# Four stacked graph-attention layers on one core: the instruction order planned anew, with other assumed durations for DMA transposes and ScalarE copies and with new due times for all layers

## The chip, the core and the metric

The kernel runs on one core of a Trainium2 chip. The metric is the device time of one execution in microseconds, the median of several runs. The engines are named as in the profile: PE (TensorE matmuls), PEld (its weight loads), DVE (VectorE), ACT (ScalarE), POOL (GpSimd) and SP (SyncE, which here only issues DMAs).

## What is computed

The input `x` has 16 batches of 1024 nodes with 256 features; `adj` is one 1024 x 1024 adjacency matrix for all of them. Four layers follow each other, each with a norm in front and a residual behind:

```python
# each layer:
h = jnp.maximum(_layernorm(x, axis=-1), 0.0)
x = x + layer(h, adj)
# layers 0 and 3 (4 heads of 64) and layer 1 (1 head of 256):
q = h @ W
e = leaky_relu(q @ a_src [node j] + q @ a_dst [node i], 0.2)   # 1024 x 1024 a head
out = elu(softmax(where(adj > 0, e, -big)) @ q)
# layer 2:
e = leaky_relu((h @ W1) @ (h @ W2).T, 0.2)
out = relu(softmax(where(adj > 0, e, -big)) @ (h @ W3))
```

Batches are independent of each other; the layers of one batch are not.

## The kernel before

**How the work is cut.** Nodes lie in 8 tiles of 128 (`NT`), queries in two halves of 512 (`HALF`). The exponential of a sum is a product, so in layers 0, 1 and 3 no 1024 x 1024 exponential is taken: a factor for each key (`ke`) and a row of factors for all queries (`row`) are combined on DVE by one instruction for 128 keys and 512 queries, which also applies the mask and gives the tile `p`. That is `weigh`, L1109 in layers 0 and 3 (64 tiles a batch and layer: 2 halves x 4 heads x 8 key tiles) and L1200 in layer 1 (16 tiles). PE then multiplies `p` with the values. In layers 0 and 3 (`steps_a`) each `p` is used by one PE step of 8 matmuls into the tile `acc`; in layers 1 and 2 (`steps_b`) a PE step takes all 8 key tiles of a half for one tile of queries, 16 matmuls into `accb`. Layer 2 computes scores on PE (`score`), takes two exponentials on ACT (`grow`, L1227 and L1228) and combines and masks on DVE (`cut`, L1232 and L1233). All matmuls in f32 go through `product`, so they all have line L575; the profile tells them apart by the tile that they write: `acc`, `accb`, or `pp` for projections, queries and scores.

After an `acc` is complete, DVE takes the reciprocal of its denominators (L1142) and the division frees the `acc`: in layer 0 on ACT (L1156), in layer 3 mostly on DVE (L1153). There are two buffers each of `acc` and `accb`, 8 of `p` for layers 0 and 3, and 18 of `p1` for layers 1 and 2.

**The way into a layer** (`prologue`). DVE takes the mean and variance of each tile of `x` (`statistics`, L815 and L816); eight such pairs belong to a batch and layer. The reciprocal root is a POOL instruction (L851) between two small ones on DVE (L848, L854). For each pair of tiles ACT then normalises (`normed`, L884, 2 instructions) and splits the f32 into two 16-bit planes (`split`, L907, 2 instructions); SP issues one DMA transpose (`move`, L911); ACT joins the planes again (`kept`, L925); PE projects (`projected`, `pp<-w,hTp` or `pp<-w2v,hT`); ACT evicts (`evict`, L960 to L969). In layers with 4 heads that aren't `filling`, DVE scales the values (L975). The factors of a layer are turned on PE (`factors`), stored to DRAM and read back as broadcast rows by SP's DMAs (L1043, L1056). The buffers between these steps are few: 4 of `h`, 2 of `planes`, 2 of `turned`, 2 of `hTp`, 4 of `pp`.

**What sets the order.** The program is laid out by a small planner, `Plan`. Each step is added with an engine, an assumed cost, a due time, the steps that it needs, and the buffers that it takes and gives. `Plan.order` (L95) plays the steps through on paper: whenever an engine is idle, it takes the ready step with the earliest due time whose buffers are free. The order in which it picks them is the order in which the instructions are emitted, so each engine's queue follows it. Costs and due times therefore change nothing but the order. The due time of a step comes from these tables (L49 to L66): `START` (when a layer of batch 0 begins, in units of `PERIOD`; batch b is b units later), `LEAD` and `AHEAD` (how much earlier the way into the layer is due), `STEP` (spacing of its four pairs of tiles), `WHEN` (layers 1 and 2: start and spacing for the tiles and for the products), `LATER` (shifts of single batches and layers), `EARLY` (how much earlier the divisions are due). Layers of neighbouring batches are in work together: in the middle of the run, layer 0 of one batch goes with layers 1, 2 and 3 of the batches before it.

The step of the DMA transpose is four plan steps, of which `landed` (L616) adds the last two:

```python
s = plan.add(ACT, 1.25, at, split, (s,), take=("planes",), give=("h", "h"))   # L932
s = plan.add(SP, 0.5, at, move, (s,), take=("turned",))
s = landed(s, at, 256, give=("planes",))         # DMA: 256 / 330 us, then LAND: 2.2 us
s = plan.add(ACT, 1.02, at, kept, (s,), take=take, give=("turned",))
```

Of the kernel before, what the change touches and what calls it, by code (L numbers as in the profile page):

```python
# [45 lines left out]

PERIOD, EARLY = 190.0, 0.74  # L49
START = {0: 0.0, 1: 0.96, 2: 2.3, 3: 3.63}  # L50
LEAD = {0: 0.7841, 1: 0.4991, 2: 0.193, 3: 1.8815}
STEP = {0: 0.028, 1: 0.0997, 2: 0.0747, 3: 0.0167}
WHEN = {
    (1, "weights"): ((-0.3, 0.04), (-0.12, 0.06)),
    (1, "attended"): ((0.56, 0.06), (0.22, 0.15)),
    (2, "weights"): ((-0.04, 0.02), (0.31, 0.02)),
    (2, "attended"): ((0.72, 0.07), (0.79, 0.02)),
}

LATER = {  # L60
    (0, 0): -0.048, (0, 1): -0.131, (1, 0): 0.06, (1, 1): 0.875, (2, 0): 0.05, (13, 2): -0.063, (13, 3): 0.612,
    (14, 2): 0.069, (14, 3): 0.042, (15, 2): -0.05, (15, 3): 1.076,
}
AHEAD = {
    (1, 0): 0.853, (2, 0): 0.078, (3, 0): 0.177, (13, 0): -0.55, (15, 2): -0.107, (15, 3): -0.22,
}  # L66


PE, DVE, ACT, POOL, SP, DMA, LAND = "PE", "DVE", "ACT", "POOL", "SP", "DMA", "LAND"
# [463 lines left out]
def fast(  # L533
# [26 lines left out]
    plan = Plan(bufs, ("p", "p1", "acc", "accb", "val4", "val1", "x", "row4", "row1"))  # L560
# [55 lines left out]
    def landed(step, due, kb, take=(), give=()):  # L616

        s = plan.add(DMA, kb / 330, due, lambda: None, (step,))
        return plan.add(LAND, 2.2, due, lambda: None, (s,), give=give)
# [133 lines left out]
    weights = ((w0, w0_ready), (w1, w1_ready), (w2v, w2v_ready), (w3, w3_ready))  # L753
# [67 lines left out]
    class Layer:  # L821
# [7 lines left out]
        def prologue(self, due, step, stats, direct=False):  # L829
# [3 lines left out]
            b, heads, layer = self.b, self.heads, self.layer  # L833
# [6 lines left out]
            ready = []  # L840
            parts = PARTS[b == 0] if direct else ((0, NT),)
            for n, its in enumerate(slice(*part) for part in parts):
# [29 lines left out]
                at = due - (len(parts) - n - 1)  # L872
                s = plan.add(DVE, 0.2, at, norm, (*stats[its], ready[-1] if n else None))
                s = plan.add(POOL, 2.0, at, norm2, (s,))
                take = () if n else (tag,) if self.gat else (tag, "hq")
                ready += [plan.add(DVE, 0.2, at, norm3, (s,), take=take)] * (its.stop - its.start)
            copies, evicted = [], []
            for n, t0 in enumerate(range(0, NT, 2)):
                at = due + n * step
# [9 lines left out]
                            scale=T["rstd"][:, t : t + 1],  # L889
                        )  # L890

                s = plan.add(ACT, 1.2, at, normed, (ready[t0],), take=("h", "h"))


                def turned(t0=t0):
# [31 lines left out]
                take = ("hTp",) if self.gat else ()  # L927
                if direct:
                    s = plan.add(PE, 0.47, at, turned, (s,), take=("pp",), give=("h", "h"), wide=True)
                    s = plan.add(ACT, 0.6, at, kept, (s,), take=take, give=("pp",))  # L930
                else:
                    s = plan.add(ACT, 1.25, at, split, (s,), take=("planes",), give=("h", "h"))  # L932
                    s = plan.add(SP, 0.5, at, move, (s,), take=("turned",))
                    s = landed(s, at, 256, give=("planes",))
                    s = plan.add(ACT, 1.02, at, kept, (s,), take=take, give=("turned",))
                copies.append(s)
                for k in range(2):
                    t = t0 + k

                    def projected(t=t, t0=t0, k=k):  # L940
                        pv = T["pv", t] = buf("pp", [P, HALF])
                        for c in range(KC):
                            product(
                                pv[:, :cols],
                                T["hT", t0][:, c, k * P : (k + 1) * P],
                                w[:, c, :cols],
                                start=(c == 0),
                                stop=(c == KC - 1),
                            )

                    s2 = plan.add(
                        PE, 0.9, at + (k + 1) * step / 3, projected, (s, w_ready), take=("pp",),
                        give=("hTp",) if k and self.gat else (),
                    )

                    def evict(t=t, many=heads > 1 and (direct or not self.filling)):
                        to = self.val[:, t, :, :d]
                        of = T["pv", t][:, :F].rearrange("p (h d) -> p h d", h=heads)
                        if not self.gat:
                            nc.scalar.copy(to, of)  # L960
                            return
                        a = self.val[:, t, :, d : d + 1]

                        nc.scalar.activation(
                            a, T["pv", t][:, F + heads : cols].unsqueeze(2), AF.Exp, scale=1.0 / (SLOPE - 1.0)
                        )
                        nc.scalar.activation(self.ke[:, :, t], T["pv", t][:, F:cols], AF.Exp)
                        for hd in range(0 if many else heads):
                            nc.scalar.mul(to[:, hd, :], of[:, hd, :], a[:, hd, :])  # L969

                    def scaled(t=t):
                        to = self.val[:, t, :, :d]
                        of = T["pv", t][:, :F].rearrange("p (h d) -> p h d", h=heads)
                        a = self.val[:, t, :, d : d + 1]
                        nc.vector.tensor_mul(to, of, a.to_broadcast([P, heads, d]))  # L975

                    many = heads > 1 and (direct or not self.filling)
                    cost = 0.4 if many or not self.gat else 0.8 if heads == 1 else 1.15
                    s2 = plan.add(ACT, cost, at, evict, (s2,), give=() if many else ("pp",))
                    if many:  # L980
                        s2 = plan.add(DVE, 0.43, at, scaled, (s2,), give=("pp",))
                    evicted.append(s2)
            at = due + 4 * step
            self.ready, self.queries = evicted, ([], [])
            if not self.gat:
                for dc in range(KC):
                    for n0 in range(0, N, HALF):
# [12 lines left out]
                        s = plan.add(PE, 1.72, at, query, (*copies, *w12_ready), take=("pp",))  # L1000
# [8 lines left out]
            if direct:  # L1009
                for half in range(2):  # L1010
                    for hd in range(heads):
# [7 lines left out]
                        def keep(half=half, hd=hd):  # L1019
# [5 lines left out]
                            take=("pp", f"row{heads}"), wide=True,  # L1025
# [20 lines left out]
            s = plan.add(PE, 0.14, at, factors, tuple(evicted), take=("pp",))  # L1046
# [141 lines left out]
    def steps_b(lay, dues):  # L1188

        T = {}  # L1190
        ready = {0: [], 1: []}
        for n in range(2 * NT):
            half, jt = divmod(n, NT)
            at = dues("weights", n)
            after = (lay.ready[jt], *mask_ready[half, jt // HT])
            if lay.gat:

                def weigh(half=half, jt=jt):
                    p = T["p", half, jt] = buf("p1", [P, HALF])
                    nc.vector.scalar_tensor_tensor(  # L1200
                        p, lay.rows[half, 0], lay.ke[:, 1, jt : jt + 1], mask_of(half, jt), op0=OP.max, op1=OP.mult
                    )

                s = plan.add(
                    DVE, 0.67, at, weigh, (*after, lay.row_ready[half, 0]), take=("p1",),
                    give=("row1",) if jt == NT - 1 else (),
                )
                ready[half].append(s)
                continue

            def score(half=half, jt=jt):
                e = T["e", half, jt] = buf("pp", [P, HALF])
                for c in range(KC):
                    product(
                        e,
                        lay.hT[:, c, jt * P : (jt + 1) * P],
                        lay.qT[:, c, half * HALF : (half + 1) * HALF],
                        start=(c == 0),
                        stop=(c == KC - 1),
                    )  # L1220


            def grow(half=half, jt=jt):
                e = T.pop(("e", half, jt))
                p = T["p", half, jt] = buf("p1", [P, HALF])
                u = T["u", half, jt] = buf("u", [P, HALF])
                nc.scalar.activation(u, e, AF.Exp, scale=1.0 - SLOPE)  # L1227
                nc.scalar.activation(p, e, AF.Exp, bias=shift_col, scale=SLOPE)  # L1228

            def cut(half=half, jt=jt):  # L1230
                p, u = T["p", half, jt], T.pop(("u", half, jt))
                nc.vector.scalar_tensor_tensor(p, u, 1.0, p, op0=OP.max, op1=OP.mult)  # L1232
                nc.vector.tensor_mul(p, p, mask_of(half, jt))  # L1233

            s = plan.add(PE, 1.72, at, score, (*lay.queries[half], *mask_ready[half, jt // HT]), take=("pp", "p1"), give=("hq",) if n == 2 * NT - 1 else ())
            s = plan.add(ACT, 1.2, at, grow, (s,), take=("u",), give=("pp",))
            ready[half].append(plan.add(DVE, 1.27, at, cut, (s,), give=("u",)))
        for it in range(NT):
            half, t = divmod(it, HT)
# [227 lines left out]
```

## Time and profile before

Three runs took 3021.66, 3022.22 and 3024.54 us; the median is 3022.22 us. The profiled execution has a span of 3023.1 us and a mean granted PE clock of 0.993.

| engine | busy us | share of the span | instructions |
|---|---|---|---|
| PE | 2929.2 | 97% | 47954 |
| DVE | 2632.4 | 87% | 5286 |
| ACT | 1926.1 | 64% | 4776 |
| POOL | 225.7 | 7% | 151 |

Busy time is the union of an engine's instructions. For PE the difference to the span, 93.9 us, is time in which no matmul runs; short gaps between pipelined matmuls don't count as idle. The profile names for each stretch of idle time the instruction that ended it. The costliest groups are L1109 (2048 instructions, 1450.8 us busy) on DVE, and on PE the products into `acc` (32768 matmuls), into `accb` (8192) and into `pp`. One DMA transpose keeps SP's queue for 1.23 us (median of 248).

### The profile page before, as it was taken

To read this page: it belongs to the slowest core of one execution; us is meant where nothing else is said; L and a number is where in the kernel's file an instruction comes from. 1 tells how busy PE (TensorE), PEld (TensorE's weight loads), DVE (VectorE), ACT (ScalarE), POOL (GpSimd) and SP (SyncE) were. 2 spreads that over 40 slices of the span, in tenths; PEclk is the share of its full clock that TensorE was granted. 3 is DMA by queue.
4 is the path that set the end of the run, shared out by engine and by line. 5 is a ranking of instruction groups with operands and counts; after the bars stand their busy time and mean duration, and the time that the engine had idled before them with its cause. 6 is when DMAs were issued, how large, how long until landed. Compare 5 with 4: busy or idle time off the path is not lost.

```text
span 3023.1 us, 108612 instructions
## 1 busy us (share of the span) xinstructions
PE 2929.2 (97%) x47954; PEld 2248.8 (74%) x47954; DVE 2632.4 (87%) x5286; ACT 1926.1 (64%) x4776; POOL 225.7 (7%) x151
## 2 busy tenths in 40 slices
PE   7899999999999999999999999999999999999997
PEld 5775888768686786867868687787867869685686
DVE  7988869989898898988979898899988979896698
ACT  6677686675656756567675656756567675547633
POOL 2110000000100000000000100001000000100000
PEclk9899999999999999999999999999999999999999
DMA  4232223213222232322323223231322323121210
GB/s 141 59 68 64 51 58 97 71 44 86 46 72 56 62 76 44 84 42 71 73 46 83 45 62 72 54 83 42 84 44 71 73 47 69 33 57 40 51 41 24
DMA packets 344047, 188.06 MB, mean 62 GB/s; under 512 B 268880, under 2 KB 304400, under 8 KB 343568
## 3 DMA queue, kind: packets, MB, share of 16 engines
q1 hardware_dynamic: 343152, 180.51, 25.9%
q8 instruction: 378, 6.19, 0.9%
q14 instruction: 101, 0.83, 0.1%
q10 hardware_dynamic: 416, 0.52, 0.1%
HBM read 98.63 MB, written 17.33 MB: 38 GB/s over the span
## 4 chain that ended last, share of the span: by engine, by line
PE 82%; DVE 14%; ACT 2%; issue 1%; DMA 0%; SPq 0%; DVEq 0%; ACTq 0%
PE pp L575 30%; PE accb L575 26%; PE acc L575 26%; DVE p L1109 8%; DVE bn L815 2%; DVE o L1080 1%; DVE mv L816 1%; DVE xt L1082 1%; DVE p L1200 1%; ACT o L1156 0%; DMA xt<-in_x_dram 0%; ACT hTp L925 0%; DVE p L1233 0%; ACT ex L1076 0%; ACT ex L1075 0%
## 5 line engine op out<-in xcount | busy, mean ns | idle before, releaser
L1109 DVE SCALAR_TENSOR_TENSOR p<-row,ke,mask 128x512 f32<-128x512 f32 x2048 | 1450.8, 762 | 69.6 <-PE acc L575 63.0
L575 PEld LDWEIGHTS acc<-val,p 128*64 128x64 f32 x32768 | 1072.9, 139 | 156.7 <-DVE p L1109 52.9
L575 PE MATMUL acc<-val,p 128*64 128x65 f32 x32768 | 1085.7, 224 | 56.9 <-DVE p L1109 45.0
L575 PE MATMUL accb<-val,p 128*64 128x257 f32 x8192 | 932.9, 380 | 0.4 <-ACT o L1265 0.4
L575 PEld LDWEIGHTS accb<-val,p 128*64 128x64 f32 x8192 | 700.2, 137 | 159.3 <-issue 3.9
L575 PE MATMUL pp<-qT,hT 128*64 128x512 f32 x2048 | 458.1, 592 | 0.0
L575 PE MATMUL pp<-w,hTp 128*64 128x264 f32 (+1 forms) x3072 | 381.1, 390 | 6.5 <-ACT hTp L925 5.4
L575 PEld LDWEIGHTS pp<-qT,hT 128*64 128x64 f32 x2048 | 149.6, 137 | 237.7 <-issue 230.9
L575 PEld LDWEIGHTS pp<-w,hTp 128*64 128x64 f32 x3072 | 240.6, 139 | 93.2 <-issue 11.4
L884 ACT ACTIVATE h<-xt,nshift,rstd 128x256 f32<-128x256 f32 x512 | 277.7, 596 | 35.7 <-DVE nshift L854 35.7
L907 ACT COPY planes<-h 128x512 uint16<-128x512 uint16 x496 | 280.8, 617 | 0.4 <-DMA turned<-planes 0.4
L1267 ACT ACTIVATE o<-accb,rdens 128x256 f32<-128x256 f32 x128 | 60.9, 475 | 344.8 <-DVE rdens L1259 341.7
L1232 DVE SCALAR_TENSOR_TENSOR p<-u,p 128x512 f32<-128x512 f32 x256 | 175.9, 687 | 117.8 <-ACT p L1228 117.8
L851 POOL TENSOR_TENSOR rstd<-rstd,neg_half 128x8 f32<-128x8 f32 (+2 forms) x67 | 124.0, 1850 | 1711.7 <-DVE rstd L848 1077.6
L925 ACT COPY hTp<-turned 128x1024 uint16<-128x1024 uint16 x184 | 212.2, 1169 | 21.0 <-DMA turned<-planes 21.0
L815 DVE BATCH_NORM_STATS2 bn<-xt 128x6 f32<-128x256 f32 x512 | 210.8, 412 | 12.2 <-DMA xt<-in_x_dram 5.2
L1227 ACT ACTIVATE u<-pp 128x512 f32<-128x512 f32 x256 | 153.7, 600 | 99.0 <-PE pp L575 93.0
L1156 ACT ACTIVATE o<-acc,rden 128x64 f32<-128x64 f32 x572 | 132.8, 321 | 107.2 <-DVE rden L1142 92.0
L1233 DVE TENSOR_TENSOR p<-p,mask 128x512 f32<-128x512 f32 x256 | 181.2, 708 | 8.8
L1200 DVE SCALAR_TENSOR_TENSOR p<-row,ke,mask 128x512 f32<-128x512 f32 x256 | 179.9, 741 | 0.0
L969 ACT ACTIVATE val<-pp,val 128x64 f32<-128x64 f32 (+1 forms) x640 | 179.5, 347 | 0.0
L1228 ACT ACTIVATE p<-pp,shift_col 128x512 f32<-128x512 f32 x256 | 176.5, 689 | 0.0
(87 smaller groups left out, 1806.2 us busy)
## 6 DMA issues: line engine op xcount, KB each, us to landing
row<-er_d SPq DMA_DIRECT2D x272, 256.0 KB
xt<-in_x_dram SPq DMA_DIRECT2D x31, 512.0 KB
out_dram<-xt SPq DMA_DIRECT2D x31, 512.0 KB
raw<-in_adj_dram SPq DMA_DIRECT2D x4, 1024.0 KB
raw<-in_adj_dram SPq DMA_DIRECT2D x16, 256.0 KB
turned<-planes SPq DMA_TRANSPOSE x248
xt<-in_x_dram SPq DMA_DIRECT2D x2, 256.0 KB
w<-in_L_gnn_W_dram SPq DMA_DIRECT2D x2, 256.0 KB
```

The costliest lines, as they stand in the source:

```text
L575: nc.tensor.matmul(to[c : c + COLS], stationary[:, c : c + COLS], moving, start=start, stop=stop, skip_group_check=True,)
L815: nc.vector.bn_stats(st, x_tiles[b][:, t, :])
L884: nc.scalar.activation(h, x_tiles[b][:, t, :], AF.Relu, bias=T["shift"][:, t : t + 1], scale=T["rstd"][:, t : t + 1],)
L907: nc.scalar.copy(to[:, :, :, k, :], of)
L925: nc.scalar.copy(bits, T["tp", t0].rearrange("p s c q -> p c q s"))
L969: nc.scalar.mul(to[:, hd, :], of[:, hd, :], a[:, hd, :])
L1109: nc.vector.scalar_tensor_tensor(p, lay.rows[half, hd], lay.ke[:, lay.heads + hd, jt : jt + 1], mask_of(half, jt), op0=OP.max, op1=OP.mult)
L1200: nc.vector.scalar_tensor_tensor(p, lay.rows[half, 0], lay.ke[:, 1, jt : jt + 1], mask_of(half, jt), op0=OP.max, op1=OP.mult)
L1227: nc.scalar.activation(u, e, AF.Exp, scale=1.0 - SLOPE)
L1228: nc.scalar.activation(p, e, AF.Exp, bias=shift_col, scale=SLOPE)
L1232: nc.vector.scalar_tensor_tensor(p, u, 1.0, p, op0=OP.max, op1=OP.mult)
L1233: nc.vector.tensor_mul(p, p, mask_of(half, jt))
```

## The change

The tables of due times get other numbers, and `LATER` and `AHEAD` get entries for more batches and layers (28 and 26 instead of 11 and 6, all for batches 0 to 3 and 12 to 15). The assumed costs of five kinds of ACT steps (`normed`, `split`, `kept`, `evict`, `grow`) change. The chain of a transpose is now written out: SP is taken for 1.23 us, the transfer for 1.6 us, the landing for 0.9 us. No step is added or removed, and no tile, buffer count or instruction is changed; the instructions of all engines stand in another order.

```diff
-PERIOD, EARLY = 190.0, 0.74
-START = {0: 0.0, 1: 0.96, 2: 2.3, 3: 3.63}
-LEAD = {0: 0.7841, 1: 0.4991, 2: 0.193, 3: 1.8815}
-STEP = {0: 0.028, 1: 0.0997, 2: 0.0747, 3: 0.0167}
+PERIOD, EARLY = 190.0, 0.7407
+START = {0: 0.0, 1: 1.0372, 2: 2.297, 3: 3.5524}
+LEAD = {0: 0.7046, 1: 0.4612, 2: 0.2956, 3: 1.6786}
+STEP = {0: 0.01, 1: 0.0686, 2: 0.0892, 3: 0.0445}
 WHEN = {
-    (1, "weights"): ((-0.3, 0.04), (-0.12, 0.06)),
-    (1, "attended"): ((0.56, 0.06), (0.22, 0.15)),
-    (2, "weights"): ((-0.04, 0.02), (0.31, 0.02)),
-    (2, "attended"): ((0.72, 0.07), (0.79, 0.02)),
+    (1, "weights"): ((-0.5242, 0.0026), (-0.1464, 0.0419)),
+    (1, "attended"): ((0.7567, 0.0147), (0.2574, 0.106)),
+    (2, "weights"): ((-0.0331, 0.0103), (0.3531, 0.0135)),
+    (2, "attended"): ((0.642, 0.0926), (0.4636, 0.0079)),
 }
...
-                s = plan.add(ACT, 1.2, at, normed, (ready[t0],), take=("h", "h"))
+                s = plan.add(ACT, 1.05, at, normed, (ready[t0],), take=("h", "h"))
...
-                    s = plan.add(ACT, 1.25, at, split, (s,), take=("planes",), give=("h", "h"))
-                    s = plan.add(SP, 0.5, at, move, (s,), take=("turned",))
-                    s = landed(s, at, 256, give=("planes",))
-                    s = plan.add(ACT, 1.02, at, kept, (s,), take=take, give=("turned",))
+                    s = plan.add(ACT, 1.1, at, split, (s,), take=("planes",), give=("h", "h"))
+                    s = plan.add(SP, 1.23, at, move, (s,), take=("turned",))
+                    s = plan.add(DMA, 1.6, at, lambda: None, (s,))
+                    s = plan.add(LAND, 0.9, at, lambda: None, (s,), give=("planes",))
+                    s = plan.add(ACT, 1.1, at, kept, (s,), take=take, give=("turned",))
...
-                    cost = 0.4 if many or not self.gat else 0.8 if heads == 1 else 1.15
+                    cost = 0.32 if many or not self.gat else 0.65 if heads == 1 else 1.05
...
-            s = plan.add(ACT, 1.2, at, grow, (s,), take=("u",), give=("pp",))
+            s = plan.add(ACT, 1.12, at, grow, (s,), take=("u",), give=("pp",))
```

## The prediction

> **What bounds the kernel now.** I read the busy times first, then PE's waits, then PE's idle time by stage, and last the timeline at the waits that come back.
>
> ```profile
> PE 2929.2 (97%) x47954; PEld 2248.8 (74%) x47954; DVE 2632.4 (87%) x5286; ACT 1926.1 (64%) x4776; POOL 225.7 (7%) x151
> ```
>
> PE is the bound: 93.9 us of 3023.1 are without a matmul. A new order removes no work, so it can win some of these 93.9 us at most, and what they consist of decides. The list of what PE waited for:
>
> ```profile
> PE acc L575 <- DVE p L1109: 45.0, 40, 4.3
> PE pp L899 <- ACT h L884: 11.8, 1, 11.8
> PE acc L575 <- ACT o L1156: 9.1, 11, 1.2
> PE pp L575 <- ACT hTp L925: 5.4, 5, 2.4
> PE pp L575 <- ACT hT L925: 4.7, 5, 1.9
> ```
>
> (Total us, times, longest.) Half is for L1109's tiles on DVE; 11.8 us are the start. The same by stages, from the busy times of windows (window, its us, busy us of PE, PEld, DVE, ACT, POOL, then PE's clock):
>
> ```profile
> 0.00:300.00 300.00, 257.39 (x4376) 191.74 (x4378) 258.39 (x527) 207.35 (x590) 43.62 (x38) 0.94 0.33 84
> 300.00:540.00 240.00, 237.48 (x3479) 198.72 (x3477) 193.26 (x401) 165.39 (x423) 14.45 (x9) 1.00 0.29 71
> 540.00:1080.00 540.00, 529.95 (x8808) 399.05 (x8806) 479.56 (x987) 351.93 (x860) 36.88 (x24) 1.00 0.27 60
> 1080.00:1262.15 182.15, 179.08 (x2986) 138.34 (x2984) 162.09 (x327) 117.44 (x288) 13.08 (x8) 1.00 0.29 63
> 1262.15:2640.00 1377.85, 1360.21 (x22466) 1049.42 (x22464) 1233.68 (x2465) 888.89 (x2165) 98.56 (x60) 1.00 0.28 62
> 2640.00:2940.00 300.00, 297.44 (x4348) 214.25 (x4346) 234.45 (x454) 165.27 (x364) 11.50 (x9) 1.00 0.22 48
> 2940.00:3023.00 83.00, 67.67 (x1511) 57.32 (x1506) 70.95 (x131) 29.85 (x90) 7.59 (x4) 0.93 0.07 22
> ```
>
> PE idles 42.6 us in the fill (to 300), 35.8 in the middle (2.5 + 10.1 + 3.1 + 17.6 + 2.6, from 300 to 2940) and 15.3 in the drain. The middle has a period of 182.15 us a batch, of which 3.07 are idle. The 179.08 busy us of a period are the work itself: 128 `acc` steps of 0.467 us (the chain has 4.20 us for x144, which is 9 steps with their weight loads), 16 `accb` steps and 20 scores and queries of 3.48 and 1.74, 32 projections of 0.88 and three `factors` of 0.15 make 178.9. So in the middle only the idle 35.8 us can be won.
>
> What they are, the timeline of batch 8's layer 0 shows twice:
>
> ```profile
> 1104.80 0.18 ACT L964 ACTIVATE val<-pp 128x4 f32<-128x4 f32 x1 [0.37 <-PE pp L575]
> 1104.87 0.18 ACT L967 ACTIVATE ke<-pp 128x8 f32<-128x8 f32 x1
> 1104.92 0.93 ACT L1156 ACTIVATE o<-acc,rden 128x64 f32<-128x64 f32 x4
> 1105.91 1.62 PE L575 MATMUL acc<-val,p 128*64 128x65 f32 x48 [1.16 <-ACT o L1156]
> ...
> 1118.12 0.39 DVE L815 BATCH_NORM_STATS2 bn<-xt 128x6 f32<-128x256 f32 x1
> 1118.55 0.18 DVE L816 BATCH_NORM_AGGREGATE mv<-bn 128x2 f32<-128x6 f32 x1
> 1119.08 2.07 DVE L1109 SCALAR_TENSOR_TENSOR p<-row,ke,mask 128x512 f32<-128x512 f32 x3
> 1119.88 0.69 PE L575 MATMUL acc<-val,p 128*64 128x65 f32 x16 [1.00 <-DVE p L1109]
> ```
>
> At 1105.91 PE needs one of two `acc` buffers; the division that frees it stood in ACT's queue behind evictions of PE's own latest projections. At 1119.88 PE needs a `p`; its L1109 stood behind the eight statistics of the next batch's `x`. Neither engine was short of time over the period; the order was wrong locally.
>
> **What the Trainium skill says.** "Trainium Kernel Development and Optimization", Performance Expectations: "matmul busy time (the `TensorMatrix` row) is a bad metric", as matmuls are pipelined. The trace agrees in part: in the middle, busy time and counted work agree within 0.2 us a period (179.08 and 178.9), so idle time is a good measure here; in the fill it isn't (below). "PSUM — Partial Sum Buffer", Engine vs sequencer instructions: the queues of ScalarE, VectorE and GpSimd are strict FIFO. The two places above agree. "TensorE: Matmul & The Clock Gate", Part 1: an idle window of about 3.4 us halves PE's clock. The fill agrees: with waits of up to 4.3 us the clock is 0.94 there. "DMA: Bandwidth & Descriptors", Anatomy of one DMA: some 2.0 us fixed a DMA. The trace has no landing of a transpose, but from its issue to the copy that waits for it there are 3.1 to 6.1 us, median 4.3 of 27; I use 4.3.
>
> **The change part by part.** All parts act through the order alone, so I cost them together, by stage, from the instruction order of both built programs, where counts are exact. One row each: L1109 holds DVE for 0.66 us when the next follows (x3 in 2.07 us with 0.74 for one), a statistics pair 0.55.
>
> *How I count.* Take a PE step that needs something from DVE or ACT, and go back in that engine's queue to an instruction that itself had to wait for an earlier PE step. Between the two the other engine has so much work in its queue, PE so much in its own. If the engine's sum, with 0.3 us for the two hand-overs (an allowance of mine), is above PE's sum, PE waits for the difference at least.
>
> *The middle.* Before, the largest shortfalls of a batch are 2.8 us at one place and 0.4 at another through DVE, and 1.4 through ACT; they overlap, and the trace has 3.07 us of idle time a batch there. The rule thus finds the waits that exist. In the new order it finds one of 0.5 us near 540 us and none from there to the drain; in a batch of the middle the nearest is 0.6 us of slack through DVE, 0.4 through ACT. The two places as examples. Before, between two L1109 there are 9 statistics pairs (5.0 us), two L975 (0.66), an L1080 with L1082 (0.91) and three small ones (0.25), 6.8 us, while PE has an `acc` step, `factors` and an `accb` step, 4.1 us; the ready `p` tiles cover part. After, three of the next batch's eight statistics stand earlier among other L1109; the gap with the other five is longer, 8.5 us, but stands beside 10.95 us of PE (two `accb` steps, four projections, one `acc`). On ACT, the division (L1156) now stands ahead of the evictions.
>
> *Transposes and SP.* 248 of 1.23 us and the row loads (0.32 us) are the same; they stand elsewhere in SP's queue. Counted with 4.3 us from issue to copy, the nearest projection after 400 us has 0.7 us of slack; before, some were short by up to 6. A transpose would be held if a row load ahead of it waited for its buffer; by the queues, none is held by more than 1.1 us.
>
> Of the 35.8 us I take 31. Work that hides the moved steps: PE's own, as counted. The rest, 5 us (0.4 a batch), is for slacks of 0.4 to 0.7 us that landing times (3.1 to 6.1 us) can eat. Bounds: 35.8 and 18.
>
> *The fill.* PE can't be faster than DVE there: layer 0 has 64 L1109 of 0.66 against 64 steps of 0.467. DVE's work ahead of a PE step, less PE's own, is at most 27.6 us before and 24.6 after, as layer 2 of batch 0 (PE-heavy) now begins inside layer 0 of batch 2. The count through ACT is 1 us worse (6.5 against 5.4). I take 3 us; bounds 7 (some of the clock returns too) and a loss of 4.
>
> *The drain.* The last 64 steps (batch 15, layer 3) stand alone as before: 49.6 us of DVE against 32.4 of PE before, 50.0 after; the same shortfall of 10.7. I take a loss of 1; bounds 0 and 3.
>
> Sum: 3023.1 - 31 - 3 + 1 = 2990.1 us of span. The median of the runs is 0.9 below this span: **2989 us**.
>
> **The rivals.** *Half is given back* (3005 us): slacks of under 1 us in the middle turn into waits, 18 us are won there. For it: landings scatter by 3 us. Against: DVE and ACT have 20 and 65 idle us a period to catch up.
>
> *Nothing comes of it* (3022 us): the waits only change places, each place with its own new shortfall. For it: the median of PE's waits is small, and nothing else is removed. Against: the count, which finds the old ones and no new ones.
>
> *Slower* (3041 us): SP's queue. SP waited 933.6 us in 165 row loads for L1109 to free a row, 24.2 at most. If in the new order a transpose stands behind such a load, projection and all later PE work wait. The point is 33 us over 12.8 periods, 2.6 us a batch; at 4 us a batch it costs 52: 2989 + 52. For it: the slack of transposes is the smallest of all. Against: the hold of 1.1 us that the queues give.
>
> **How the numbers follow.** The forecast has 0.76 (2979 to 2998), half given back 0.12, nothing 0.03, slower 0.05; 0.04 for still faster, if the fill gives more. Range: from 3022 - 35.8 - 7 = 2979 to 3005, the middle of the half case; it leaves out some 0.18. About 0.2% (6 us) is what a measurement of this kernel can tell from no change. Faster by more: 0.76 + 0.12 + 0.04 = 0.92; same 0.03; slower 0.05.
>
> **What would show it.** Right: PE's idle time from 300 to 2940 us falls from 35.8 to about 5; the wait of `acc` for L1156 (9.1 us) goes; that for L1109 falls from 45.0 to some 27, nearly all before 240 and after 2940; the distance of equal places of batches falls from 182.15 to about 179.5 us. The fill's idle time stays within 4 us of 42.6, the drain's 15.3 within 3. Wrong: a wait of PE for L925 in every batch (transposes), an idle time before 300 above 50, or a busy time of PE well over 2929 us, as then matmuls themselves run slower.

## The result and the profile after

The changed kernel takes **2978.76 us** (median of 4 runs, 2978.35 to 2980.5) against 3022.08 for the kernel before in the same comparison (3021.66 to 3024.54): a ratio of 0.9856, 95% interval 0.9839 to 0.9873. The forecast was 2989, its range began at 2979. The sign was right and most of the gain lies where it was forecast, but 10 us more were won than forecast (13 by the profiled spans: 2990.1 forecast, 2977.1 measured), and the low end, which should have been a bound, was passed by 0.2 us.

Lines below the tables have moved by 7 or 8: L575 is now L582, L1109 is L1117, L1156 is L1164, L1089 is L1097, L815 is L822. First the busy times, and the list of what PE waited for (total us, times, longest):

```profile
PE 2911.8 (98%) x47954; PEld 2321.2 (78%) x47954; DVE 2645.6 (89%) x5286; ACT 1922.3 (65%) x4776; POOL 234.5 (8%) x151
```

```profile
PE acc L582 <- DVE p L1117: 33.8, 34, 8.3
PE pp L906 <- ACT h L891: 11.9, 1, 11.9
PE acc L582 <- ACT o L1164: 3.9, 1, 3.9
PE pp L582 <- ACT hTp L932: 2.1, 4, 0.9
```

The waits for the division (9.1 us, 11 times) are gone but for one, and those for transposed copies (L925 before, in two tiles 10.1 us together) are 2.1. The surprise stands in the first row: PE's **busy** time fell from 2929.2 to 2911.8 us with the same 47954 matmuls. A new order was to move idle time only. The windows (window, its us, busy us of PE, PEld, DVE, ACT, POOL, then PE's clock):

```profile
0.00:300.00 300.00, 260.65 (x4586) 201.52 (x4588) 266.65 (x540) 206.95 (x596) 42.57 (x36) 0.95 0.35 84
300.00:540.00 240.00, 239.71 (x3589) 193.01 (x3586) 207.16 (x432) 170.85 (x423) 17.09 (x12) 1.00 0.32 72
540.00:1080.00 540.00, 538.16 (x8851) 434.29 (x8847) 485.58 (x990) 369.85 (x905) 39.03 (x24) 1.00 0.29 64
1080.00:2640.00 1560.00, 1553.11 (x25840) 1238.00 (x25838) 1418.92 (x2818) 1005.84 (x2459) 114.16 (x69) 1.00 0.28 63
```

Between 300 and 2640 PE now idles 9.0 us (0.3 + 1.8 + 6.9). Before 300 it idles 39.35, only 3.3 less than the 42.6 of before; yet in these 300 us it runs 4586 matmuls where it ran 4376. So PE did more in nearly the same busy time. How, the timeline of PE and DVE in the fill shows (start, us, then the instructions that follow each other without a gap):

```profile
106.15 6.02 DVE L1117 SCALAR_TENSOR_TENSOR p<-row,ke,mask 128x512 f32<-128x512 f32 x9
106.92 5.42 PE L582 MATMUL acc<-val,p 128*64 128x65 f32 x128 [0.16 <-DVE p L1117]
```

These 128 matmuls are 8 PE steps (the 8 matmul calls of a step stand as 16 in the profile). At the free pace of 0.467 us a step they need 3.7 us; they took 5.2 (5.42 less the 0.22 by which a matmul's modelled end lies behind its start), 0.65 a step. That is the pace of L1117, 0.66 a tile: PE waited for DVE in each step, and no gap is shown, because the modelled end of the last matmul covers the 0.19 us of waiting. **Busy time hid waits.**

So I count a second quantity besides idle time: for each PE step, the time from its start to the start of the next in the trace, less idle time, less what such a step takes unhindered (0.467 for `acc`, 3.482 for `accb`, 1.717 for scores and queries, 0.88 for projections: medians of neighbouring equal steps). This is the *stretch*. Idle and stretch together are PE's loss. With the stages cut at equal PE work (230 and 2820 us of it, so that the same steps are compared), in us:

| loss, idle + stretch | fill | middle | drain |
|---|---|---|---|
| before | 29.3 + 30.2 = 59.5 | 35.5 + 16.3 = 51.8 | 8.4 + 10.2 = 18.6 |
| after | 25.8 + 20.8 = 46.6 | 9.4 + 7.8 = 17.2 | 8.9 + 11.0 = 19.9 |
| difference | -12.9 | -34.6 | +1.3 |

The sum, -46.2, is the difference of the spans (3023.1 to 2977.1) within 0.2; the 11.8 us of start, the last 8 us and 2874 us of PE work are the same in both. The medians differ by 43.3 only: the profiled run of the kernel before took 3024.89 us, 2.8 above its median, so some 3 us of these 46 belong to that run and not to the change.

A likely reason why the fill gives 12.9 stands in DVE's waits there. From 20 to 180 us, of the kernel before:

```profile
DVE o L1080 <- ACT ex L1076: 4.9, 4, 2.5
DVE rden L1142 <- PE acc L575: 4.5, 4, 2.2
DVE rden L1259 <- PE accb L575: 3.0, 1, 3.0
DVE val L975 <- ACT ke L967: 2.7, 3, 1.3
DVE p L1109 <- ACT mask L743: 2.6, 1, 2.6
```

and of the changed kernel:

```profile
DVE rden L1150 <- PE acc L582: 2.9, 3, 1.1
DVE val L983 <- ACT ke L975: 1.3, 3, 0.5
DVE o L1088 <- ACT ex L1084: 1.3, 1, 1.3
DVE p L1117 <- PE acc L582: 1.0, 2, 0.6
```

With the smallest row (0.4 in both) DVE waited 18.1 us before and 6.9 after. Where PE runs at DVE's pace, what DVE loses in a wait for ACT or PE can come back as PE's loss later. This is argued; the table below supports it only roughly.

### The profile page after: what moved, and what is told of

It reads as the page before. It is cut to its first block, busy times and chain, and to the rows that moved or that the text cites. A ratio compares the mean times of both kernels' runs of the same rounds, so it can differ in the third digit from the quotient of the medians.

```text
span 2977.1 us, 108647 instructions
## 1 busy us (share of the span) xinstructions
PE 2911.8 (98%) x47954; PEld 2321.2 (78%) x47954; DVE 2645.6 (89%) x5286; ACT 1922.3 (65%) x4776; POOL 234.5 (8%) x151
## 4 chain that ended last, share of the span: by engine, by line
PE 84%; DVE 12%; ACT 1%; issue 1%; DMA 0%; POOL 0%; SPq 0%; DVEq 0%; POOLq 0%
PE pp L582 31%; PE accb L582 27%; PE acc L582 26%; DVE p L1117 8%; DVE o L1088 1%; DVE bn L822 1%; DVE xt L1090 0%; DVE p L1241 0%; DVE mv L823 0%; DVE p L1240 0%; DMA xt<-in_x_dram 0%; ACT hTp L932 0%; POOL xt L1097 0%; DMA turned<-planes 0%; DVE rden L1150 0%
## 5 line engine op out<-in xcount | busy, mean ns | idle before, releaser
L1117 DVE SCALAR_TENSOR_TENSOR p<-row,ke,mask 128x512 f32<-128x512 f32 x2048 | 1460.3, 768 | 34.2 <-PE acc L582 32.6
L582 PEld LDWEIGHTS acc<-val,p 128*64 128x64 f32 x32768 | 1072.4, 139 | 121.6 <-issue 47.3
L582 PE MATMUL acc<-val,p 128*64 128x65 f32 x32768 | 1074.5, 223 | 38.9 <-DVE p L1117 33.8
L582 PE MATMUL accb<-val,p 128*64 128x257 f32 x8192 | 928.0, 380 | 0.0
L582 PEld LDWEIGHTS accb<-val,p 128*64 128x64 f32 x8192 | 734.4, 136 | 131.6 <-issue 4.1
L582 PE MATMUL pp<-qT,hT 128*64 128x512 f32 x2048 | 461.4, 592 | 0.0
L582 PE MATMUL pp<-w,hTp 128*64 128x264 f32 (+1 forms) x3072 | 380.8, 386 | 3.3 <-ACT hTp L932 2.1
L582 PEld LDWEIGHTS pp<-qT,hT 128*64 128x64 f32 x2048 | 171.1, 137 | 211.9 <-issue 209.2
L582 PEld LDWEIGHTS pp<-w,hTp 128*64 128x64 f32 x3072 | 242.5, 137 | 85.2 <-issue 12.0
L822 DVE BATCH_NORM_STATS2 bn<-xt 128x6 f32<-128x256 f32 x512 | 211.8, 414 | 13.3 <-DMA xt<-in_x_dram 5.4
L1164 ACT ACTIVATE o<-acc,rden 128x64 f32<-128x64 f32 x572 | 132.2, 316 | 113.4 <-DVE rden L1150 99.9
L1097 POOL TENSOR_TENSOR xt<-xt,o 128x1024 f32<-128x1024 f32 x35 | 97.5, 2785 | 1131.7 <-DVE o L1088 1009.6
```

What stands on the lines that cost most here:

```text
L582: nc.tensor.matmul(to[c : c + COLS], stationary[:, c : c + COLS], moving, start=start, stop=stop, skip_group_check=True,)
L822: nc.vector.bn_stats(st, x_tiles[b][:, t, :])
L1117: nc.vector.scalar_tensor_tensor(p, lay.rows[half, hd], lay.ke[:, lay.heads + hd, jt : jt + 1], mask_of(half, jt), op0=OP.max, op1=OP.mult)
L1164: nc.scalar.mul(to[:, t, :], acc[:, t, :d], rden[:, t, :])
```

## The experiments

Loss by stage as above; "DVE waits" are those from 20 to 180 us. e5 adds matmuls, so its loss has no like to compare. Each ratio is to the kernel before on the same chip. The kernel before took 3022.1 to 3025.4 us in these comparisons, so times of different rows compare within some 3 us only.

| kernel | us | ratio, 95% interval | fill | middle | drain | DVE waits |
|---|---|---|---|---|---|---|
| before | 3022.08 | | 59.5 | 51.8 | 18.6 | 18.1 |
| after | 2978.76 | 0.9839 to 0.9873 | 46.6 | 17.2 | 19.9 | 6.9 |
| e1_costs_only | 3005.77 | 0.9920 to 0.9953 | 47.5 | 48.7 | 16.6 | 13.7 |
| e2_tables_only | 3001.99 | 0.9907 to 0.9940 | 52.3 | 39.0 | 17.6 | 13.9 |
| e9_act_costs | 2989.49 | 0.9867 to 0.9900 | 55.0 | 22.4 | 17.5 | 18.6 |
| e10_transpose_costs | 3024.38 | 0.9992 to 1.0010 | 55.7 | 54.5 | 16.7 | 14.4 |
| e3_stats_later_act | 2998.64 | 0.9900 to 0.9933 | 57.9 | 26.8 | 18.3 | 16.9 |
| e7_stats_later | 3001.63 | 0.9907 to 0.9940 | 57.8 | 30.2 | 18.5 | 17.0 |
| e4_layer2_late | 2985.00 | 0.9852 to 0.9885 | 47.8 | 22.9 | 20.6 | 8.3 |
| e6_layer2_early | 3025.66 | 0.9991 to 1.0009 | 63.2 | 47.9 | 18.3 | 16.9 |
| e5_kept_warm | 2978.43 | 0.9834 to 0.9866 | | | | |
| e8_pool_add_on_dve | 2956.48 | 0.9758 to 0.9790 | 41.9 | 4.8 | 15.2 | 5.8 |
| e11_before_add_on_dve | 3008.37 | 0.9932 to 0.9965 | 53.1 | 43.8 | 17.1 | 15.8 |

In the fill e7 has the order of before (its edit begins with batch 4) and loses 57.8 where before loses 59.5: some 1.7 us in the fill is what two profiles of one order differ by.

**Which half carries the gain: the costs or the due times?** e1 is the changed kernel with the tables of before (from `PERIOD` to `AHEAD`), e2 the kernel before with the new ones; each table goes over as the diff of the change shows it.

```diff
...
-LEAD = {0: 0.7046, 1: 0.4612, 2: 0.2956, 3: 1.6786}
+LEAD = {0: 0.7841, 1: 0.4991, 2: 0.193, 3: 1.8815}
...
```

> The planner's new costs with the old due times. Theory A (the gain of the middle comes from where the due times put DVE's and ACT's steps; the costs matter only as far as the new due times were fitted to them): the shortfalls counted in the queues of this order are as large in the middle as before (DVE 22 against 30, ACT 20 against 23), so the span stays within 12 us of before, 3010 to 3030, and the waits of PE for L1109 and for copies come back in every batch. Theory B (the true duration of the DMA transposes and copies is what repairs the order): most of the 45 us comes with the costs alone, 2980 to 2995.

> The new due times with the planner's old costs. Theory A: most of the gain stays; the counted shortfalls of the middle are 8 (DVE) and 9 us (ACT) in all, against 0.5 and 0 with the new costs, so 2985 to 3000, 5 to 20 us slower than the full change. Theory B: near the kernel before, 3005 to 3025.

Neither theory holds. The costs alone give some 18 us, 12.0 of them in the fill, the tables alone some 22, in both stages (7.2 and 12.8). Together they give 43. Neither half alone mends the middle: it loses 48.7 and 39.0 with one half, 17.2 with the whole. That all of both is not needed for it, e9 shows below.

**The two places of the middle, mended by hand.** The prediction named the eight statistics ahead of L1109 and the division behind the evictions. e7 spaces the statistics in the kernel before; e3 also pulls each division on ACT ahead of the evictions that directly precede it, in the finished order (of all batches, so ACT's order differs in the fill too):

```diff
-            stats = [statistics(b, t, due, (loads[b][t],)) for t in range(NT)]
+            stats = [statistics(b, t, due + (4.0 * t if b > 3 else 0.0), (loads[b][t],)) for t in range(NT)]
...
+            while kind.get(on[first - 1]) == "evict":
+                first -= 1
...
+            if first < n:
+                res.remove(k)
+                res.insert(res.index(on[first]), k)
```

> The kernel before with two local repairs from batch 4 on: the due times of the eight statistics of the next x are spread by 4 us each, and the division of layer 0 is put ahead of evictions of projections that stand directly before it on ACT. Fill and drain as before. Theory A (local order of these two is what PE waits for in the middle): the counted shortfalls of the middle fall from 30 to 6 (DVE) and from 23 to 5 (ACT), PE idles about 10 us less than 26 of the 35.8 us from 300 to 2940, and the busy time of PE falls too, by 5 to 9 us, because the waits under 0.15 us go with them: 2990 to 3000. Rival (the waits only move to the next shortage): over 3012. Rival on the busy time (it is the matmuls themselves that run faster in the new order, not hidden waits): the idle time falls but the busy time from 300 to 2940 stays within 2 us of before.

> Only the first of the two local repairs: the statistics of the next x due 4 us apart from batch 4 on, the ACT order as planned. Counted shortfalls in the middle: DVE 6 (30 before), ACT 10 (23 before). If each repair wins its own waits, some 60 to 80 per cent of the 26 us that both won: 3001 to 3007. If PE waits for whichever of the two is later, little: over 3012.

The idle time of the middle falls from 35.5 to 12.5 us with the statistics alone and to 9.4 with both, the value of the changed kernel. So the named waits were the idle time. But the stretch stays (16.3 before, 17.7 and 17.4), so the forecast that the busy time falls with them fails: hand-mended waits leave the hidden ones, which the new order also lowers, to 7.8. The rival that was named for this case, matmuls that run faster in the new order, does not fit either: in the middle two neighbouring `acc` steps start 0.467 us apart in the median before, after and in e3. The stretch sits in few of them (58 of 1323 hold 8.7 us before, 26 of 1353 hold 4.6 after).

**Layer 2 begun earlier in the fill.** The prediction put the fill's gain down to layer 2 of batch 0 beginning inside layer 0 of batch 2. e4 takes that shift out of the changed kernel, e6 puts it alone into the kernel before (one entry each of a longer line).

```diff
-    ... (14, 3): -0.089, (0, 2): -0.137, (12, 2): 0.2,
+    ... (14, 3): -0.089, (0, 2): 0.02, (12, 2): 0.2,
```

```diff
-    (0, 0): -0.048, (0, 1): -0.131, ...
+    (0, 2): -0.137, (0, 0): -0.048, (0, 1): -0.131, ...
```

> The changed kernel with layer 2 of batch 0 due at 2.317 periods in place of 2.160, where it stood before (2.300): its scores then run after most of layer 0 of batch 2. Theory C (the 13 us that the fill won come from layer 2 of batch 0, PE-heavy, filling PE inside layer 0 of batch 2, when DVE is short): at least half is lost, 2985 to 2995. Theory D (they come from the earlier part of the fill, before 180 us, from the order of layer 0 of batches 0 and 1, and from less time at half clock): 2976 to 2983.

> The kernel before with layer 2 of batch 0 due 26 us earlier, so that its queries and scores stand ahead of the first products of layer 0 of batch 3; nothing else is set. Theory C in its narrower form (before, batch 3's layer 0 stood in front of them, and PE followed DVE between 216 and 251 us, 5.7 us of loss): that loss goes, and those 5 to 6 us stay won in the time: 3015 to 3019. Theory D (a fill bounded by DVE before that point, with the loss only moved): within 2 us of before at 300 us, 3020 to 3025.

Without the shift the fill loses 47.8 against 46.6, a difference within what two profiles of one order show; the 6 us by which e4 is slower are lost in the middle (22.9 against 17.2), so its time reaches theory C's range for another reason, which is open. But **neither run tests the reason**. In e4 layer 2's scores still begin before layer 0 of batch 2 ends (234.9 against 260.9 us). In e6 they begin after it, as they do in the kernel before (262.3 us, where that layer 0 ends at 246):

```profile
241.61 1.57 PE L575 MATMUL acc<-val,p 128*64 128x65 f32 x48
...
247.94 3.68 PE L575 MATMUL pp<-w2v,hT 128*64 128x256 f32 x16 [4.66 <-ACT hT L925]
251.41 7.51 PE L575 MATMUL pp<-hT,w 128*64 128x512 f32 x32
258.75 3.60 PE L575 MATMUL pp<-qT,hT 128*64 128x512 f32 x16
```

The first line ends layer 0 of batch 2; the last two are layer 2's queries and scores. The shift only put them ahead of batch 3's products, where PE waited for layer 2's copies, so the fill loses 3.7 us more than before and the time is the same. The traces do limit the reason. The changed kernel has done 150 us of PE work at 206.7 us, the kernel before at 214.1, and layer 2's first query runs at 210.1 us in the changed kernel. Some 7 of the 12.9 us are thus won before layer 2 begins and must have another cause; for the other 5 or so the reason is untested.

**PE's clock in the fill.** e5 adds 100 small matmuls ahead of batch 1's first product in the changed kernel, into a part of `acc` that isn't read, so that PE idles less there:

```diff
                     acc = buf("acc", [P, HALF])
+                    for _ in range(100 if (lay.b, lay.layer, half, hd) == (1, 0, 0, 0) else 0):
+                        nc.tensor.matmul(
+                            acc[:, 384:512], ident_b, ident_b, start=True, stop=True, skip_group_check=True
+                        )
```

> The changed kernel with 100 extra small bf16 matmuls ([...]their results are overwritten by the product that follows, so the output stays) in the one long wait of the fill: in front of batch 1's first product, where PE stood idle for 8.3 us and ran at half clock for the 13.7 us after 92.9. Clock theory (part of what the fill won is less time at half clock): full clock after 97 us, the products of batch 1 at 0.66 us or less in place of 0.87, and the loss of the fill 2 to 4 us smaller: 2975 to 2977. DVE theory (PE follows DVE there, whatever its clock): the same clock effect, but the loss of the fill within 1.5 us of the changed kernel's: 2978 to 2980.

The granted clock from 60 to 120 us rose from 0.86 to 0.94 (the 13.7 us at half clock from 92.9 us became 3.4), and PE's wait for L1117 before 300 fell from 22.0 to 17.2 us, as the added matmuls fill it. But DVE's tiles `p` start within 0.22 us of the changed kernel's before 210 us and within 0.04 from 210 to 400 us, and the time is 2978.43 against 2978.76. Half clock cost nothing at this place, where DVE sets the pace. The 10.2 us at half clock from 188.4 us are in both runs, and what they cost is not tested.

**Which of the costs.** e9 has only the five new ACT costs, e10 only the new chain of the transpose; both have the old tables (of e9's five lines the first is shown).

```diff
-                s = plan.add(ACT, 1.2, at, normed, (ready[t0],), take=("h", "h"))
+                s = plan.add(ACT, 1.05, at, normed, (ready[t0],), take=("h", "h"))
...
```

```diff
-                    s = plan.add(SP, 0.5, at, move, (s,), take=("turned",))
-                    s = landed(s, at, 256, give=("planes",))
+                    s = plan.add(SP, 1.23, at, move, (s,), take=("turned",))
+                    s = plan.add(DMA, 1.6, at, lambda: None, (s,))
+                    s = plan.add(LAND, 0.9, at, lambda: None, (s,), give=("planes",))
```

> The kernel before with only the five assumed ACT costs of the change (normed, split, kept, evict, grow); the chain of the transpose and all tables are before's. With all new costs the time was 3005.8 us, 18 below the kernel before, of which some 12 in the fill. Theory ACT: the order of the fill is set by what the planner believes ACT can do, as ACT feeds DVE there with its pairs of copies; these costs alone then give 3005 to 3013 us, with the lost time at 180 us of PE work at 57 to 63 us (71.3 before). Theory SP: the believed time of the transposes decides; then ACT's costs alone leave 3018 to 3026 us and some 68 to 72 us lost.

> The kernel before with only the new chain of the DMA transpose (SP 1.23 us, transfer 1.6 us, landing 0.9 us); ACT's assumed costs and all tables are before's. Theory SP: 3005 to 3013 us, of which 8 to 13 us are won in the fill. Theory ACT: 3017 to 3026 us, with the lost time at 180 us of PE work within 3 of 71.3 us. By the instruction order I hold ACT for the likelier: this edit moves about a third as many PE rows as the other.

Theory SP fails: the transposes' costs alone give nothing. Theory ACT names the right costs but neither the size nor the place: ACT's costs alone give 35 us where at most 19 were expected, the most of any part, and 29.4 of them in the middle. Set beside e1, adding the transposes' costs to ACT's loses 16 us again while the tables are old. How e9 wins, PE's part of its timeline shows:

```profile
1089.37 1.15 PE L575 MATMUL acc<-val,p 128*64 128x65 f32 x32
1090.31 3.70 PE L575 MATMUL accb<-val,p 128*64 128x257 f32 x32
1093.79 3.78 PE L575 MATMUL pp<-w,hTp 128*64 128x264 f32 x32
1097.35 2.08 PE L575 MATMUL acc<-val,p 128*64 128x65 f32 x64
1099.21 3.70 PE L575 MATMUL accb<-val,p 128*64 128x257 f32 x32
```

From 1089.0 to 1101.2 DVE makes no `p` for layer 0: the eight statistics still stand together without an L1109 between them, and this gap (12.2 us) is longer than the one of before (7.1 us, at 1112), with six `p` in reserve at the start of both. But here PE has two products into `accb` and four projections beside it, and idles nowhere. In the middle, e9's waits for L1109 are 3.4 us in all, where before has 13.9, and those for L1156 0.3, where before has 9.1. The prediction's "the order was wrong locally" was right; that the statistics had to be taken apart would have been wrong. Moving PE's other work beside them does as well.

**The residual addition on POOL.** In the trace single L1109 take four times their length. One place in the kernel before, on both engines:

```profile
136.34 5.50 DVE L1109 SCALAR_TENSOR_TENSOR p<-row,ke,mask 128x512 f32<-128x512 f32 x5
```

```profile
136.50 2.80 POOL L1089 TENSOR_TENSOR xt<-xt,o 128x1024 f32<-128x1024 f32 x1 [19.40 <-DVE o L1080]
```

Five L1109 in 5.50 us instead of 3.4: one of them takes 2.85 us, as long as POOL's addition beside it. Over 2 us take 19 of the 2048 L1109 of the kernel before and 24 L1117 of the changed kernel, each of them beside one of POOL's 35 additions. e8 has the 35 additions on DVE in the changed kernel, e11 in the kernel before, in an unchanged order (in e11 the same edit at L1081 and L1089):

```diff
-                if not on_pool:
-                    nc.vector.tensor_add(xs(), xs(), o)
+                nc.vector.tensor_add(xs(), xs(), o)
...
-                s = plan.add(POOL, 2.7, due, lambda: nc.gpsimd.tensor_add(xs(), xs(), T["o", key]), (s,), give=gives)
+                s = plan.add(POOL, 2.7, due, lambda: None, (s,), give=gives)
```

> The changed kernel with the 35 residual adds of L1097 on DVE right after L1088 in place of POOL; the plan's order is kept. In the trace one L1117 next to each of these adds takes 2.85 us in place of 0.74, so POOL's add costs DVE 2.1 us, the same add on DVE 1.22 us. If POOL holds DVE up, DVE wins 0.9 us for each of the adds that lie in the DVE-bound fill and drain (9 of 35) and PE's 3.9 us wait for the division behind the 7.5 us add at 2923 us goes: 2967 to 2975. If those long L1117 are only long in the profile (DVE idle or its end modelled), DVE gets 35 times 1.22 us more work, 2979 to 2990.

> The kernel before with the 35 residual additions of L1089 on DVE in place of POOL, in an unchanged order. In the changed kernel this move gave 22.3 us, of which 8 in the middle, where 9 us of idle time were left. Theory lock: each POOL addition holds one L1109 about 2 us longer, which costs PE where DVE has nothing ready, in any order; the gain is then as large or larger in the old order, 18 to 30 us, so 2994 to 3006 us, and the fill's loss falls by 4 to 9 us. Theory order: in the old order the waits at the statistics and at the divisions come first and hide it, so the gain is under 8 us, 3016 to 3024 us, with the middle's idle time still 30 us or more.

e8 takes **2956.48 us**, 22 below the changed kernel and more than expected; it beats both kernels. The weigh instruction of the changed kernel and of e8 (shortest, median, longest of 2048, in ns; first and last start):

```profile
L1117 DVE SCALAR_TENSOR_TENSOR p<-row,ke,mask x2048: 708/745/2877, 25.8 to 2968.3; 128x512 f32<-128x512 f32 x187
```

```profile
L1116 DVE SCALAR_TENSOR_TENSOR p<-row,ke,mask x2048: 715/744/1224, 26.1 to 2946.5; 128x512 f32<-128x512 f32 x187
```

The longest falls from 2877 to 1224 ns and the sum of all from 1460.3 to 1411.1 us, so DVE's busy time falls by 19 us although it does 35 additions of 1.2 us more. e11 lies between its two theories: 16 us, 6.4 in the fill as the lock has it, but 8.0 in the middle, where the idle time stays at 29.4 us. The additions on POOL cost some 16 to 22 us in both orders: they are no part of the change's gain, and the changed kernel leaves this cost in. In e8 the middle loses 4.8 us in all, so most of what the changed kernel still lost there, 17.2, hung on them.

## Why the prediction missed

Of the 13 us or so by which the forecast span was missed, 9.9 are the fill's and 3.6 the middle's; the drain's 0.3 go the other way.

**The middle: "the busy 179.08 us of a period are the work itself ... only the idle 35.8 us can be won".** This step failed. 26.1 us of idle time went where 31 were forecast, and 8.5 us of stretch, which the step said could not exist; that their sum, 34.6, comes near to 31 is in part luck. The period is 178.8 to 178.9 us now, below the "work". The agreement of 179.08 with a counted 178.9 was a coincidence of two errors: the durations that I counted with were rounded up from rows that hold modelled ends (1.74 where steps follow each other in 1.717 us, 0.15 for `factors` where the starts are 0.056 apart, 0.7 us a period), and the stretch of before is 16.3 us over some 14 periods, 1.1 a period. The warning that the prediction cites from the Trainium skill ("Trainium Kernel Development and Optimization", Performance Expectations, busy time is a bad metric) was right for the middle too; that agreement made me set it aside.

**The fill: "I take 3 us; bounds 7".** This step failed too, and its term was mis-sized most: 12.9 us were measured. The count of DVE's work ahead of PE's (27.6 to 24.6 us) held DVE's queue as never idle, and DVE waited 18.1 us there before and 6.9 after, 11.2 us less. That these waits are what PE won fits in size but is not shown. The reason given for the 3 us, layer 2's earlier start, cannot hold for some 7 of the 12.9, which are won before layer 2 begins; for the rest e4 and e6 do not test it. The clock, which the bound of 7 allowed for, is worth nothing at the place that e5 tests. Which step of the fill frees DVE stays open: ACT's costs alone and the transposes' alone take 4.5 and 3.8 us from the fill's loss, both together 12.0, the tables alone 7.2, and DVE's waits follow the loss only roughly (e1 and e2 have nearly the same waits and differ by 4.8 us in loss; e9 waits as long as before and loses 4.5 less). That the fill's idle time would stay "within 4 of 42.6" came true, 39.35, which shows that it measured the wrong thing.

**The drain: a loss of 1.** Measured 1.3, less than two profiles of one order can differ by, and with a cause that was not foreseen: the agreement is luck. The timeline of the changed kernel near its end:

```profile
2922.82 7.49 POOL L1097 TENSOR_TENSOR xt<-xt,o 128x1024 f32<-128x1024 f32 x1 [15.17 <-DVE o L1088]
...
2930.34 0.93 ACT L1164 ACTIVATE o<-acc,rden 128x64 f32<-128x64 f32 x4 [8.72 <-POOL xt L1097]
2931.32 0.92 PE L582 MATMUL acc<-val,p 128*64 128x65 f32 x12 [3.93 <-ACT o L1164]
```

One POOL addition took 7.49 us (2.8 is the median of the 35), ACT waited for it with the division that frees `acc`, and PE lost 3.9 us; without POOL's additions (e8) the drain loses 15.2 instead of 19.9. Why this one took so long is open.

**What held.** The division's wait is gone from the middle, and PE waits for transposed copies 2.1 us in all, so nothing of the rival that would have been slower, transposes held in SP's queue, shows in PE's waits. The counting rule (the other engine's queue between two hand-overs against PE's own) found the visible waits and put the orders in the right rank, not in the right sizes: its shortfalls in the middle, through DVE and ACT, are 30 and 23 us before, 22 and 20 in e1, 8 and 9 in e2, 6 and 10 in e7, 6 and 5 in e3, 0.5 and none after; the losses are 51.8, 48.7, 39.0, 30.2, 26.8 and 17.2. The wait for L1117 is 33.8 us instead of "some 27", as 6.9 us of it stay between 300 and 2895.

**The range.** Its low end summed two bounds, 35.8 and 7. The first left out the stretch, though the middle's 34.6 stayed inside it; the second is what was passed, by the fill's 12.9. The case "half is given back" was also summed wrong: with 18 us won in the middle, 3 in the fill and 1 lost in the drain it is at 3002 us, not 3005.

## What to carry to other kernels

Where two engines hand tiles over one by one, busy time can hold waits: compare the distance of starts with the free pace before a bound is set at the idle time. If one engine sets another's pace in a stage, read the first one's waits too; its losses can become the second's. And a better assumed cost in a planner need not give a better order: one set gave 35 us, the other nothing, and both with the old due times 18.

## What the runs showed of the hardware

A POOL addition of two SBUF tiles (128x1024 f32, 2.8 us) can hold up the DVE instruction beside it for as long as it runs. In the changed kernel 24 of 2048 L1117 take over 2 us, 2.85 in the median, where 0.74 is usual, and each stands beside one of the 35 additions; without these additions the longest of all takes 1.22 (e8). Not every DVE instruction is held: beside the addition at 918.9 us of the changed kernel, the statistics keep their usual 0.4 us. The Trainium skill has the rule in "SBUF — State Buffer", SBUF: two separate sides: DVE and GpSimd share a pair of ports under an exclusive lock, which a DVE operation with two SBUF inputs also takes against a GpSimd operation that reads SBUF. The runs agree and give the price of this kernel's 35 additions: 22 us of 2979 (e8) and 16 of 3024 (e11), though POOL is busy for 8% of the span only and stands in no row that PE waited for. PE at half clock, on the other hand, cost nothing at the one place where it was tested: 13.7 us became 3.4, and the time stayed (e5).
